# Output products of nine units from float32 with sums to three one-pass products of split halves, in a cross-attention kernel on one Trainium2 core

## The chip, the core and the metric

The kernel runs on one core of a Trainium2 chip (trn2). The metric is the device time in microseconds of one execution. Five engines work beside each other, each through its own queue in order: TensorE (PE, matrix products into the PSUM banks; weight loads are listed apart as PEld), VectorE (DVE), ScalarE (ACT), GpSimd (POOL) and SyncE (SP, which here only issues transfers).

## The reference

Inputs are `x` [2, 2048, 640], a context [2, 128, 384] and eight weights. The last 4 context rows are the adapter's tokens, the first 124 the text.

```python
query = hidden_states @ Wq
hs = _mha(query, enc @ Wk, enc @ Wv)              # 8 heads of 80, 124 text keys
ca_q1 = einsum('btc,th->bch', ca, Wq_ca)[:, indices, :]   # 384 channels spread to 2048
ca_hs1 = _mha(ca_q1, residual, residual)          # 2048 x 2048 scores, 384 distinct rows
ca_hs2 = _mha(ca_hs1 @ Wq, ca @ Wk_ca, ca @ Wv_ca)  # 4 keys
out = (hs + ca_hs2) @ Wout + b_out + residual
```

All of it is float32. The part that changes is the last line's product with `Wout`, [4096, 640] by [640, 640].

## The kernel before, in words

The 4096 tokens are cut into 8 blocks of 512 (for queries) and 16 units of 256 (for scores, probabilities and output); unit `m` is the second half or the first of block `m // 2`. The stages that matter here are these.

The adapter (`adapter`, `contract`, `second`) runs one chain per batch: scores `s` into a four-bank PSUM tile, a maximum on DVE (`mx`), scores again the other way round, an exponential on ACT (`ea`), and an accumulation `acc` on PE against `y_sb`. Only after the second batch's last `acc` are `y_sb` and the four-bank tile free; the latter becomes four more PSUM banks, eight in all.

For each unit, `text_scores` forms scores `sc` from the queries, `softmax` makes probabilities that go out to DRAM and come back turned (`kept`, then `pT`), `hidden` forms the hidden rows `ph` (three groups: chunks 0 and 1, chunks 2 and 3, chunk 4) from `pT` and the values, and `text_out_fast` multiplies them with `Wout` in steps `po`, each of which DVE adds to the residual rows (`x_more` or `last_rows`, which already hold `x` plus the bias). `stored` writes the rows out.

`text_out_fast` treats two token tiles by two pairs of 128-row chunks by two column halves of 320 as a 2x2 block product and forms it with seven products in place of eight, from sums of the hidden rows (`s1` to `s4`, on DVE or POOL) and of `Wout` (`wout_sums`, four tiles in the room of `Wq`, made once after the last query). The fifth chunk is multiplied plainly, four products. A product is two chunks wide for the seven, one for the fifth. Every product is float32. `Desk.matmul` issues a float32 product that fills the array as four strips of 32 columns, unless the instruction before filled the whole array; the printed records show each strip as two instructions. The last unit's last chain is split in two halves of 160 columns, each stored by itself.

Room limits: the hidden rows of a unit with their sums take one of three sets (`hs_sets`), and `pT` has two buffers, both made from tiles that earlier stages give up.

The order of all work is written out by hand of a planner: `ORDER` is a list of task numbers, one for each step, with a letter (`a`, `v`, `g`) where the engine is chosen there. `Desk.run` walks it and pins each instruction at its place in its engine's queue. Generators (`text`, `adapter` and so on) yield the steps; a `Room` is a count of free buffers, and a step that takes one from it can only stand in the order after the step that gives it. So `ORDER` sets the queues; waits between engines are semaphores made from the tiles that instructions read and write.

Of the kernel before, what the change touches and what calls it, by code (L numbers as in the profile page):

```python
# [45 lines left out]
class Do:  # L46
# [4 lines left out]
    def __init__(self, engine, fn, after=None, needs=(), frees=(), marks=()):  # L51
        self.engines = (engine,) if isinstance(engine, str) else engine
        self.fn, self.after, self.needs, self.frees, self.marks = fn, after, needs, frees, marks
        self.slots, self.value = [], None
# [12 lines left out]
class Desk:  # L67
# [3 lines left out]
    SIDES = {"a": "ACT", "v": "DVE", "g": "POOL"}  # L71
# [3 lines left out]
        2 2 2 2 2 2 36 0 0 0 4 4 0 0 0 0 0 0 0 0 4 0 0 111a 6 6 6 0 4 6 4 2 2 2 2 2 2 2 4 113a 107 108 109 110 4 6  # L75
        114a 115a 3 6 3a 3 116v 4 6 3a 3 3v 6 3 8 8 7 7 7 2 15 15 15 11 15 15 12 8 7 0 0 118a 8 5 15 15 15 15 10 7
        117a 15 7 8 7 7 7 120a 9 1 119v 8 6 121a 7 7 7 7 122a 7 7 124v 9 123v 125a 126a 8 8 127 8 9 8 36 5 128 8 8 8 5
        9 9 9 129 5 130 15 36 15 15 131 9 9 14 14 9 14 14 14 14 9 14 6 112 136a 133a 135v 134v 14g 137 36 112 11 112
        15 14 15 36 14 12 14g 36 138 138 138 36 138 138 12 12 12 36 144v 145v 12 36 36 11a 9 9 9 139 11 9 9 9 140 143a
        9 146a 12 13 101 17 106 140 140 140 140 141 18 6 140 140 140 140 142 106 132 132 16 17 147g 148g 132 101v 142  # L80
        132 101v 101g 101g 101g 39 152 152 152 152 152 152 151 17 17 36 36 156a 142 142 142 18 18 18 18 18 18 18 18
        132 142 16 151 152 36 36 142 16 16 157a 43 151 152g 149g 152 16 132 16 101v 101 18 16 16g 36 159 159 16 36 158
        36 101g 150g 101g 17 160a 159 159 16 151 161a 16g 155 18 18 18 152 162 36 153 36 18 158 158 18 158 155 17 155
        153 36 20 20 19 163 159 159 163 163 21 21 171 163 142 142 158 172 164 163 163 36 21 21 172 172 172 172 21 43
        154 36 154 175 175 165 159 36 175 175 175 175 19 19 19 159g 166g 167g 159 36 36 170 39 181a 36 170 21 21 21 21
        172 172 172 19 20 19 19 182 177 176 177 182 175 19g 19 177 177 159 173 36 20 183a 170 20 36 168g 182 182 182
        182 172 19 184a 20 178 170 178 182 169g 175g 17 21 21 21 21 21 21 22 19g 177 174 177 185 23 182g 36 36 185 185
        186a 185 185 175 24 24 24 24 24 175 24 174 174 24 24 188 24 174 187 185 36 22 47 22 22 22 192 22 180 194 179
        36 180 192 192 192 192 22 192 22g 182 190 174 182 36 179 180 36 195 192 196 36 47 174 174 174 158 20 23 202 23
        23 24 24 24 197 22 197 198g 192g 199v 36 192 36 24 201g 24 206a 197 197 197 22 200g 197 23 202 23 208 51 207a  # L90
        208 174 189 208 208 208 208 197 197g 22g 36 209 209 36 202 205 209 214a 209 192 132 197 189 158 189 189 189
        197 132 189 202 36 215a 209 205 189 209 36 216 55 36 203 205 209 217 217 24 209g 36 26 26 217 217 217 217 209
        217 27 27 27 27 27 158 209 210 27 212 27 204 36 204 203 218 51 36 36 225 224 219g 220g 222g 221g 217g 36 193
        226 226 223 228 230a 223 228 36 226 226 226 226 232a 229 193 217 132 158 217 158 189 23 189 191 191 191 191 27
        55 231v 36 36 233v 229 223 226 193 193 193 234 234 226g 36 226 235 234 234 234 234 25 26 229 234 36 236 36 36
        27 191 226 191 191 191 191 27 211 36 227 223 227 237 27 238 234g 234 25 59 239 239 25 25 27 27 27 27 239 239
        239 239 36 211 36 211 132 211 211 177 36 26 59 26 36g 241 241 211 211 211 211 213 29 29 241 241 241 247 239
        243v 240 251v 25 36 36 36 26 244g 247 36 252 252 254a 36 247 36 252 252 30 234 213 56 177 30 30 30 30 213 213
        213 25 239g 241 241 239 239 240 177 245g 241g 242 249 36 36 252 253 252 255a 253 247 249 253 253 36 253 36 25
        256v 253 36 63 252 193 252 252 40 213 28 252 36 44 30 30 30 30 193 262 262 257 246g 240 241 250 263 241 177 25  # L100
        240 213 262 262 262 262 36 67 36 36 252 213 240 30 30 30 264 30 264 30 250 252 250 36 30 262 265 262g 262 264
        264 213 36 252 252 31 252 29 31 36 252 264 264 31 36 67 36 31 193 193 258 260 193 262 259 259 10 259 36 60 26
        33 33 33 33 252 252 252 29 36 29 252 29 32 268 32 31 33 267 267 33 33 259 266 266 259 264 264g 269g 270g 264
        266 266 36 266 266 268 36 36 268 268 268 63 252 266 252 252 252 252 276 268 276 266v 267 31 33 264 267 274 273
        276 276 252 282a 36 36 36 252 273 36 283 283 284v 273 36 276 276 36 36 283 283 248 36 248 259 242 259 259 283
        283 271g 272v 276 31 242 285v 273 36 36 31 267 32 259 31 283 36 283 266 286 287v 33 31 283 28 36 31 28 28 36
        31v 252 28 283 281 71 36 283 276v 289 283 281 261 261 261 261 261 261 25 28 266 277 28 261 36 290 33 283 290
        288 33 36 281 283 290 290 36 290 290 33 291 33 276 33 33 32 36 75 28 25 276 25 36 261 283 28 35 35 68 283 283
        290 25v 292 292 290g 242 242 290 292 292 292 261 292 25 25 32 32 275 298 292 36 298 283 36 283 34 293v 294g
        25v 298 298 75 36 292g 298 298 301 295g 301 290 292 36 280 242 280 242 275 275 275 292 302 288 275 28 301 301  # L110
        301 301 28 28g 301 304 279 242 71 279 242 242 305 306 242 305 305 305 305 305 297 103 35 242 283 35 242 242
        283 283 307 288 242 102 275 68 296g 66 66 31 31 31g 36 36 275 275 275 299 68 68 28 11 310v 301v 307 35 242 64
        314 29 283 314 283 28 35 315 301 314 28g 316 283 48 283 283 309 317a 242 242 297 309 283 313 242 313 318a 313
        242 314 314 309 313 297 316 316 305 242 242 288 288 301 10 305g 32 316 278 278 278 316 313a 320a 308 297 308
        316 305 242 323 319 242 324 242 34 34 34 34 313 325 68 68 68 105 103 104 104 267 48 79 242 332 242 48 48 34 46
        46 278 34 321 34 278 305 332 311g 328g 330g 329g 68 68 335a 68 242 336a 331g 312g 339g 340g 333g 341g 338g 34
        102 105 40 38 38 34 48 48 40 48 278 68 288 337a 332 332 332 332 79 242 344 242 348 332 344 242 346 348 346 344
        344 242 242 345 344 242 344 344 348 278 348 34 348 278 278 348 52 332g 332 347 344 242 345 83 242 349 349 242
        349 349 349 349 345 345 349 347 48 242 352a 48 48 48 334g 359 34g 242 242 300 44 300 34 332 40 40 40 44 44 40
        300 44 44 44 351 288 300 300 349g 355g 349 349 288 42 240 240 42 34 354a 353a 356g 34g 357g 343g 358g 342g 242  # L120
        360 83 242 360 360 365 359 365 242 365 365 365 365 359 359 362 362 365 242 361 359 242 242 300 104 361 360 359
        242 40 359 40 44 242 359 365g 363g 40 367a 300 40 300 369a 368a 300 372g 365 373g 371a 87 348 242 380 380 44
        242 242 242 381a 44 384v 374v 380 382a 380 380 52 44 242 242 242 380 364g 385g 375g 376 376 378 377 387 378
        387 376 387 387 376 379 387 376 379 288 240 50 52 288 52 240 242 52 242 52 242 242v 242 366 240 365 52 50 377
        380 380g 348g 393g 392g 327 387 376 242 377 387 376 242 242 242 391 303 303 303 303 303 380 377 376 327 267
        387 327 327 380 267 391 52 52 242 391 391 242 52 52 327 391 60 327 396v 397v 403 303 303 386v 383v 403 399v
        400g 401v 242 398a 91 407 407 242 391 303 303 322 35 64 391 407 407 407 407 403 391 242 389 407 327 395 403
        403 403 242 242 242 391 322 327 267 322 267 322 322 327 402v 407g 407 407 391 403 404 242 389 403 242 91 64 60
        327 64 64 391 322 391 391 391 242 404 404 408 408 348 322 408 408 242 408 408 404 390 348 64 64 58 409 370 408
# [53 lines left out]
    def run(self):  # L183
        for entry in self.ORDER.split():
# [7 lines left out]
            for room, i in op.frees:  # L192
                room.give(i)
            for k in op.marks:
                self.event(k).known = True
# [44 lines left out]
def kernel(  # L240
# [1897 lines left out]
    for m in range(UNITS):  # L2138
        begin(text(m))
# [33 lines left out]
```

## Time and profile before

| | |
|---|---|
| median of 3 runs | 566.56 us (564.76 to 568.67) |
| span of the profiled execution, first to last instruction | 562.6 us |
| PE busy | 554.5 us, 99% |
| DVE, ACT, POOL busy | 386.4, 265.7, 198.4 us |
| granted TensorE clock | 1.000 |
| moved by transfers | 101.48 MB |

The profile is of one execution. Its own time is not listed beside its span; the median of the runs is 4.0 us above the span. A record of PE lasts from its start to a modelled end, and records overlap; so the distance from one start to the next tells what an instruction costs when PE is full. A row of a group gives line, engine, operation, `out<-in` with the shapes and a count, then the busy time, the mean duration of one in ns, and the idle time of the engine just before with what ended it. `128*32` is rows by columns of the array that an instruction uses. float32r operands are printed as f32 on PE and as fp32r where another engine writes them.

### The profile page before, as it was taken

The numbers are of one execution on the slowest core, as the hardware profiler recorded it, in microseconds if no ns is written. First come the engines' busy times: TensorE is split into PE (matmuls) and PEld (weight loads), VectorE is DVE, ScalarE is ACT, GpSimd is POOL, SyncE is SP. The second block draws the span as 40 slices with busy tenths as digits, with TensorE's granted clock in tenths as the row PEclk, the third lists the DMA queues.
The fourth block names the chain that finished last, engine by engine and source line by source line (L and its number), as shares of the span: only waits on it lengthen the run. The fifth ranks groups of instructions, "written<-read, shape, count | busy, mean of one in ns | idle before, by whom it ended". The sixth has DMA issues, their size and how long they took to land.

```text
span 562.6 us, 18845 instructions
## 1 busy us (share of the span) xinstructions
PE 554.5 (99%) x8088; PEld 314.4 (56%) x8088; DVE 386.4 (69%) x622; ACT 265.7 (47%) x733; POOL 198.4 (35%) x211
## 2 busy tenths in 40 slices
PE   9999999999999999999999999999999999999997
PEld 8563445456555555555465445455545666666664
DVE  1457999999996564579999998655635655555534
ACT  3122645445338898886525424579878230100100
POOL 7002534434524523013559364512330513321310
PEclk9999999999999999999999999999999999999999
DMA  8994769774877889455568895758853687688603
GB/s 264 240 172 127 154 119 161 165 169 141 162 198 163 179 249 172 140 170 172 170 138 248 217 236 133 241 163 255 252 165 108 181 186 192 150 262 229 203 28 142
DMA packets 151699, 101.48 MB, mean 180 GB/s; under 512 B 86492, under 2 KB 130156, under 8 KB 151616
## 3 DMA queue, kind: packets, MB, share of 16 engines
q1 hardware_dynamic: 150848, 99.88, 69.6%
q8 instruction: 64, 1.05, 0.8%
q0 software_dynamic: 768, 0.40, 0.4%
q14 instruction: 19, 0.16, 0.1%
HBM read 61.34 MB, written 38.90 MB: 178 GB/s over the span
## 4 chain that ended last, share of the span: by engine, by line
PE 91%; DVE 3%; DMA 3%; ACT 1%; SPq 1%; POOL 1%; issue 0%; ACTq 0%; DVEq 0%
PE po L211 26%; PE pq L211 25%; PE acc L211 8%; PE sc L211 7%; PE ph L211 7%; PE s L211 7%; PE pq_first L211 3%; PE pyz L211 3%; DVE mx L226 2%; PE pk L211 1%; PE unread L215 1%; DMA zb<-z 1%; DMA x_more<-in_x_dram 1%; DMA first_rests<-away 1%; SPq L236 1%; PE pt_wq L219 1%
## 5 line engine op out<-in xcount | busy, mean ns | idle before, releaser
L226 DVE TENSOR_REDUCE mx<-s 128x4 f32<-128x2048 f32 x48 | 109.2, 2275 | 2.5 <-PE s L211 2.4
L226 ACT ACTIVATE p<-sc,m 128x124 f32<-128x124 f32 x256 | 89.5, 374 | 32.2 <-DVE m L226 32.2
L226 ACT ACTIVATE ea<-s 128x2048 f32<-128x2048 f32 x48 | 90.4, 1884 | 26.5 <-PE s L211 26.2
L226 POOL TENSOR_TENSOR p<-p,r 128x992 f32<-128x992 f32 x28 | 51.9, 1857 | 132.9 <-DVE r L226 126.1
L211 PE MATMUL po<-wout_sums,hs 128*32 128x320 f32 (+1 forms) x1012 | 77.8, 433 | 0.5 <-DVE x_more L226 0.5
L211 PE MATMUL po<-wout_sb,hs 128*32 128x320 f32 (+2 forms) x972 | 77.1, 429 | 0.0
L226 DVE TENSOR_TENSOR x_more<-x_more,po 128x320 f32<-128x320 f32 x72 | 33.7, 480 | 42.6 <-PE po L211 42.6
L226 ACT ACTIVATION_READ_ACCUMULATOR p<-sc,m 128x1 f32 x256 | 55.4, 217 | 0.0
L211 PE MATMUL pq<-xt,wq_sb 128*32 128x256 f32 x896 | 54.3, 381 | 0.5 <-DVE q L226 0.5
L211 PEld LDWEIGHTS po<-wout_sums,hs 128*32 128x32 f32 (+1 forms) x1012 | 37.5, 110 | 29.7 <-issue 1.6
L211 PEld LDWEIGHTS po<-wout_sb,hs 128*32 128x32 f32 (+1 forms) x972 | 36.7, 111 | 27.4 <-issue 0.9
L211 PE MATMUL acc<-ea,y_sb 128*32 128x384 f32 (+2 forms) x768 | 50.4, 384 | 0.0
L226 DVE TENSOR_REDUCE m<-sc 128x4 f32<-128x496 f32 x64 | 40.8, 663 | 13.6 <-PE sc L211 13.4
L226 POOL TENSOR_TENSOR hs<-hs 128x256 f32<-128x256 f32 x35 | 27.5, 790 | 63.5 <-DVE hs L226 54.7
L211 PE MATMUL ph<-pT,vpad 128*32 128x256 f32 x768 | 46.7, 380 | 0.2 <-ACT p L226 0.2
L226 DVE TENSOR_TENSOR last_rows<-last_rows,po 128x320 f32<-128x320 f32 (+1 forms) x57 | 26.4, 473 | 24.8 <-PE po L211 24.7
L226 DVE STREAM_TRANSPOSE eb<-p 128x1024 f32<-128x1024 f32 x32 | 39.5, 1234 | 5.3 <-POOL p L226 3.3
L211 PEld LDWEIGHTS pq<-xt,wq_sb 128*32 128x32 f32 x896 | 27.5, 110 | 22.9 <-issue 5.5
L226 ACT COPY hs<-ph 128x512 f32<-128x512 f32 (+1 forms) x23 | 12.1, 541 | 58.9 <-PE ph L211 58.6
L211 PE MATMUL pq<-xt,wq 128*32 128x512 f32 x320 | 38.8, 595 | 0.0
L211 PEld LDWEIGHTS sc<-kmain,q 64*128 64x128 f32 x512 | 31.8, 187 | 11.9 <-issue 7.5
L211 PE MATMUL sc<-kmain,q 64*128 64x124 f32 x512 | 37.5, 283 | 0.2
(197 smaller groups left out, 792.3 us busy)
## 6 DMA issues: line engine op xcount, KB each, us to landing
kept<-eb SPq DMA_DIRECT2D x32, 512.0 KB
pT<-kept SPq DMA_DIRECT2D x48, 256.0 KB
landing<-away SPq DMA_DIRECT2D x60, 128.0 KB
xi<-in_x_dram SPq DMA_DIRECT2D x28, 256.0 KB
x_more<-in_x_dram SPq DMA_DIRECT2D x18, 320.0 KB
out_dram<-x_more SPq DMA_DIRECT2D x18, 320.0 KB
last_rows<-in_x_dram SPq DMA_DIRECT2D x14, 320.0 KB
y<-yt SPq DMA_DIRECT2D x16, 256.0 KB
```

Source lines behind the costliest of these rows:

```text
L211: self.pin(self.nc.tensor.matmul(out[strip], lhsT[:, strip], rhs, **kw))
L215: self.pin(self.nc.tensor.matmul(out, zeros, zeros, start=True, stop=True))
L219: self.pin(self.nc.tensor.transpose(out, in_, ident))
L226: return lambda *args, **kw: self.pin(getattr(engine, what)(*args, **kw))
L236: self.pin(self.nc.sync.dma_start(out, in_))
```

## The change

Units 0 to 4, 6 and 7 (`BY_SUMS`) keep `text_out_fast`, without the split at the end. Units 5 and 8 to 15 use the new `text_out`. Each float32 number is split in a top part of 12 bits and a remainder; both are float32r, which PE multiplies in one pass. With `top`, `low` (the remainder) and `mix` (their difference, scaled), three products give the full product: top by top, low by low, mix by mix, all accumulated in one bank and scaled once when DVE adds them to the residual. `Wout` is split by `wout_part` in five chunks of [128, 640], five steps each; the parts lie in rooms that the adapter's `zop`, `y_sb`, `yz`, the late tiles and `kmain` give up. The hidden rows are split in `hidden_parts` when they leave PSUM. An output of 128 tokens by 320 columns is one step of 15 matmuls, four such steps a unit, and no float32r matmul is cut into strips.

`hs_sets` goes from three sets to two; three sets of parts (`k_sets`) are added, one from two query slots, two more when the seven units by sums are done. `pT` gets two further buffers, from the tiles `ea0` and `ea1`, when the second batch's adapter rows are out. Bookkeeping (what marks a step done, when a room grows) is moved from side effects into steps of their own, which issue nothing. In `halves_away` both ACT copies now come ahead of both DVE subtractions. `ORDER` is new from end to end, 2366 entries for 2241; it was laid out by the planner with disturbed timings.

```diff
     def matmul(self, out, lhsT, rhs, **kw):
         rows, cols = lhsT.shape
-        wide = rows > 64 and cols > 64 and self.mode != (P, P)
+        wide = rows > 64 and cols > 64 and self.mode != (P, P) and lhsT.dtype == F32
...
+    BY_SUMS = (0, 1, 2, 3, 4, 6, 7)
+    UNDER, UP, DOWN = 1.0 - 2.0**-13, 2.0**12, 2.0**-12
+    ACROSS = -DOWN / (1.0 + DOWN)
...
-        yield from text_out_fast(m)
+        yield from (text_out_fast if m in BY_SUMS else text_out)(m)
...
     def take_pT():
...
+        yield Do("NONE", lambda *z: None, [("o2", B - 1)], needs=[(eas, 2)], grows=[(pTs, 2)])
...
+    def wout_parts():
...
+        yield Fork(one(Do("NONE", lower, [("acc done", B - 1, u) for u in range(2)], marks=["wout lows"])))
...
+        yield Fork(one(Do(
+            "NONE", mixed_in, ["wout lows"] + [("sc", m, k) for m in range(UNITS) for k in range(2)],
+            needs=[(yzs, 1)], marks=["wout mixes"],
+        )))
...
+    def wout_part(c):
+        top = w_parts["top"][c]
+        yield Do(ANY, lambda: top_of(top, wout_sb[:, c]), marks=[("wout top", c)])
+        op = yield Do(
+            ADDS, lambda: minus(w_parts["low"][c], wout_sb[:, c], top.bitcast(F32)), ["wout lows", ("wout top", c)],
+        )
+        low = w_parts["low"][c]
+        yield Do(ANY, lambda: times(low, UP), marks=[("wout up", c)])
+        yield Do(
+            ADDS, lambda: minus(w_parts["mix"][c], top.bitcast(F32), low.bitcast(F32)), ["wout mixes", ("wout up", c)],
+        )
+        yield Do(ANY, lambda: times(w_parts["mix"][c], ACROSS), marks=[("wout mix", c)])
...
+    def hidden_parts(m, c0, n, hs, ph, s, at):
...
+        yield Do(EITHER, lambda: top_of(cols("top"), src), [at], marks=[("hs top", m, c0)])
+        yield Do(
+            "DVE", lambda: minus(cols("low"), src, cols("top", True)), frees=[(banks, s)], marks=[("hs low", m, c0)],
+        )
...
+        op = yield Do(("DVE", "ACT"), scaled)
...
+    def out_part(m, i, u, hs):
+        def product(s, kinds=("top", "low", "mix")):
+            po = bank(s[0], f"po_{m}_{i}_{u}")
+            steps = [(k, c) for k in kinds for c in range(NCH)]
+            for n, (k, c) in enumerate(steps):
+                matmul(
+                    po[:, :HALF], hs[k][c - c % 2][:, c % 2, P * i : P * (i + 1)],
+                    w_parts[k][c][:, HALF * u : HALF * (u + 1)],
+                    start=(n == 0), stop=(n == len(steps) - 1),
                 )
...
+            desk.v_scalar_tensor_tensor(t, po[:, :HALF], 1.0 + DOWN, t, ALU.mult, ALU.add)
```

In `hidden_parts`, `scaled` writes `mix` in one DVE step (`low` times -4096 plus `top`), or `low` times 4096 on ACT with a subtraction on POOL or DVE behind it.

More of the change, by code (lines that the diff above doesn't have):

```diff
@@ L1170, in queries_fast @@
         )
[L1171 to L1184 removed]
+        yield Fork(read_all(n))
         def chain(n, c, steps):
@@ new lines, in times, with lower, mixed_in @@
+    def times(t, factor):
+        if desk.engine == "ACT":
+            desk.a_activation(t, t.bitcast(F32), AF.Identity, scale=factor)
+        else:
+            (desk.g_tensor_scalar if desk.engine == "POOL" else desk.v_tensor_scalar)(
+                t, t.bitcast(F32), factor, None, ALU.mult
+            )
+    ANY, ADDS = ("ACT", "DVE", "POOL"), ("POOL", "DVE")
+    def wout_parts():
+        yield Do("NONE", lambda: None, [("zop", B - 1, sb, 1) for sb in range(NSB)])
+        tops, lows, mixes = w_parts["top"], w_parts["low"], w_parts["mix"] = [], [], []
+        def lower():
+            t = const.tile([P, 6, H], F32R, tag="y_sb", name="wout_low")
+            lows.extend(chunks(t[:, :NCH]))
+            mixes.append(t[:, NCH])
+        yield Fork(one(Do("NONE", lower, [("acc done", B - 1, u) for u in range(2)], marks=["wout lows"])))
+        def mixed_in(y):
+            mixes.extend([
+                cap.tile([P, H], F32R, tag="yz", name="wout_mix_1"),
+                late["pool"].tile([P, H], F32R, tag="rests", name="wout_mix_2"),
+                late["pool"].tile([P, H], F32R, tag="landing", name="wout_mix_3"),
+                const.tile([P, H], F32R, tag="kmain", name="wout_mix_4"),
+            ])
+        yield Fork(one(Do(
+            "NONE", mixed_in, ["wout lows"] + [("sc", m, k) for m in range(UNITS) for k in range(2)],
+            needs=[(yzs, 1)], marks=["wout mixes"],
+        )))
+        for c in range(NCH - 1):
+            yield Do(
+                "NONE", lambda z, c=c: tops.append(cap.tile([P, H], F32R, tag=f"zop{z[0]}", name=f"wout_top_{c}")),
+                needs=[(zops, 1)],
+            )
+            yield Fork(wout_part(c))
+        yield Do(
+            "NONE", lambda: tops.append(const.tile([P, H], F32R, tag="wq4", name="wout_top_4")), ["last query"]
+        )
+        yield Fork(wout_part(NCH - 1))
@@ L2027, in text_out_fast @@
         one_h, both_h, end_h = of1, of2, [("hsT", m, 4)]
-        left = {"sums": 8, "products": 4}
         ready = [("xr", m, k) for k in range(2)]
@@ L2053, in product @@
                     return to
+                end = k == len(steps) - 1
                 op = yield Do(
-                    "PE", product, after + at + ready, needs=[(banks, 1)] if k == 0 else []
+                    "PE", product, after + at + ready, needs=[(banks, 1)] if k == 0 else [],
+                    marks=[("products", m, n)] if end else [],
                 )
@@ L2095, in stored @@
+    ends = {}
+    spans = (0, HALF), (HALF, H), (0, H)
     def stored(m, k, u, added):
```

443 lines of the change are left out of this document (260 added, 183 removed).

## The prediction

> **What bounds the kernel now.** I read the page first, for the engine that is never free.
>
> ```profile
> span 562.6 us, 18845 instructions
> PE 554.5 (99%) x8088; PEld 314.4 (56%) x8088; DVE 386.4 (69%) x622; ACT 265.7 (47%) x733; POOL 198.4 (35%) x211
> PE 91%; DVE 3%; DMA 3%; ACT 1%; SPq 1%; POOL 1%; issue 0%; ACTq 0%; DVEq 0%
> PE po L211 26%; PE pq L211 25%; PE acc L211 8%; PE sc L211 7%; PE ph L211 7%; PE s L211 7%; PE pq_first L211 3%; PE pyz L211 3%; DVE mx L226 2%; PE pk L211 1%; PE unread L215 1%; DMA zb<-z 1%; DMA x_more<-in_x_dram 1%; DMA first_rests<-away 1%; SPq L236 1%; PE pt_wq L219 1%
> ```
>
> TensorE (PE) is busy for 99% of the span and carries 91% of the chain of waits; the largest single item on that chain is `po`, the output products that the change rewrites. Busy is not the same as streaming, so the table by stage comes next. I cut it at 437 us, where the last adapter work ends and only scores of a late tile, hidden products (`ph`) and output products (`po`) are left.
>
> ```profile
> core 0: us, PE busy (x) PEld busy (x) DVE busy (x) ACT busy (x) POOL busy (x), PEclk, DMA share, GB/s
> 45.00:180.00 135.00, 133.65 (x1988) 70.92 (x1988) 123.55 (x157) 66.64 (x251) 54.75 (x43) 1.00 0.71 156
> 180.00:345.00 165.00, 163.00 (x2425) 86.96 (x2418) 129.69 (x167) 106.11 (x280) 71.27 (x63) 1.00 0.76 190
> 345.00:437.00 92.00, 92.00 (x1453) 50.02 (x1449) 49.51 (x87) 68.74 (x143) 26.38 (x20) 1.00 0.65 187
> 437.00:559.00 122.00, 121.98 (x1885) 76.37 (x1875) 64.95 (x136) 12.73 (x38) 33.25 (x35) 1.00 0.64 178
> ```
>
> From 437 to 559 us PE has no idle time at all, VectorE (DVE) is busy 65 of 122 us, and the transfers use 0.64 of their engines. In that stage the time is PE time and nothing else. Earlier PE is as full, but DVE is at 123.55 of 135 us in the stage from 45 to 180, so that there two engines are close to their limit. How much of the output work lies in the late stage:
>
> ```profile
> 437.00:562.60 125.60, 99.81 (x1434) 58.32 (x1434) 36.49 (x81) 1.00 0.62 175
> ```
>
> This is the row of `po` alone: 1434 matmul records. One output product of 128x128 by 320 columns is issued as eight (four column strips of 32, two instructions each), so these are 179 products, ten units of 18 less one. Ten of the sixteen units do their output products after 437 us; the nine that are changed (5 and 8 to 15) are among them, and unit 4 is the tenth.
>
> **The change part by part: the products.** Price of one old product, from a stretch of the timeline with nothing in between:
>
> ```profile
> 449.75 6.13 PE L211 MATMUL po<-wout_sums,hs 128*32 128x320 f32 x88
> 455.67 1.29 PE L211 MATMUL po<-wout_sb,wout_sums 128*32 128x320 f32 x16
> 456.75 1.51 PE L211 MATMUL ph<-pT,vpad 128*32 128x256 f32 x24
> ```
>
> From 449.75 to the start of `ph` at 456.75 are 7.00 us for 104 instructions, 13 products: 0.538 us each. The strip form hides its weight loads completely. A unit had 7 sum-products of two chunks and 4 fifth chunks, 18 products: 9.69 us; nine units 87.2 us.
>
> A new unit has 4 outputs x 3 kinds x 5 chunks = 60 matmuls of full 128x128 weights by 320 columns in `float32r`. The trace has no full-array matmul of that type, so its price is put together from three sets of rows. First the streaming rate:
>
> ```profile
> L211 PE MATMUL pq<-xt,wq_sb 128*32 128x256 f32 x896 | 54.3, 381 | 0.5 <-DVE q L226 0.5
> L211 PE MATMUL pq<-xt,wq 128*32 128x512 f32 x320 | 38.8, 595 | 0.0
> L211 PE MATMUL s<-zop,cop x192: 462/497/504, 45.3 to 343.4; 32*128 32x512 f32 x192
> L211 PE MATMUL s<-cop,zop x384: 213/352/442, 177.4 to 434.4; 32*128 32x384 f32 x64, 32*128 32x128 f32 x64, 32*128 32x256 f32 x64
> ```
>
> An `f32` instruction takes 214 ns more for 256 more columns, 0.84 ns a column. The one-pass kind (`zop` and `cop` are `float32r`, which the trace prints as f32) takes at most 442 ns at 384 columns and 497 in the median at 512: 55 ns for 128, 0.43 a column, half, and an `f32` product needs two such instructions. So 320 columns stream in 133 to 138 ns. Second, whether the weight load hides under it:
>
> ```profile
> 59.81 0.66 PE L211 MATMUL sc<-krest,rests 64*128 64x124 f32 x8 [0.40 <-ACT rests L226]
> 177.43 0.51 PE L211 MATMUL s<-cop,zop 32*128 32x384 f32 x8
> L211 PE MATMUL sc<-krest,rests x256: 268/272/323, 59.8 to 443.8; 64*128 64x124 f32 x128
> ```
>
> Eight one-pass matmuls of `sc` run as four pairs, each pair with new 128-column weights: the last ends 0.66 us after the first began and itself takes 0.272, so it begins after 0.39 us. Take off the 0.05 by which the first waits longer (0.323 less 0.272), and three steps fill 0.34 us, 0.11 a step, where 124 columns stream in 0.053. The step is the load. In the second row the two rounds of `s` (384, then 128 columns) take 0.51 us: a load of 0.11, streams of 0.16 and 0.05 and the 0.16 by which a record outlasts its stream (0.213, the shortest, less the 0.053 of 128 columns) make 0.48; a second load in the open would make it 0.59. So a one-pass load costs about 0.11 us and goes on while the matmul before it streams. Third, for full-array weights:
>
> ```profile
> 34.09 3.93 PE L211 MATMUL pk<-ctxT,w_k 128*128 128x248 f32 x18
> L211 PE MATMUL pk<-ctxT,w_k 128*128 128x248 f32 x18 | 3.9, 373 | 0.0
> ```
>
> Eighteen of these, each with its own load, advance by (3.93 - 0.37)/17 = 0.209 us, and 248 columns stream in 0.208: the loads are hidden there too. With a load of 0.11 under a stream of 0.133 I take 0.136 us for a new matmul (0.133 to 0.140): 8.16 us a unit, 73.4 for nine. The products give back 87.2 - 73.4 = **13.8 us**, all of it in the stage where PE is the bound.
>
> [...]
>
> **Mode changes.** `ph` stays in 128x32 strips, so PE now goes from strips to full array and back.
>
> ```profile
> 438.17 1.26 PE L211 MATMUL po<-wout_sb,hs 128*32 128x320 f32 x16
> 439.37 0.55 PE L219 MATMUL pt_acc<-ident,accs 128*128 128x128 f32 x3
> ```
>
> Two products stream in 1.08 us from 438.17, to 439.25; the full-array transposes begin at 439.37: 0.12 lost, and the first load on top, at most 0.11. The way back costs the same drain and a load of a quarter of the columns, 0.03: up to 0.38 us a pair. In the new order the hidden products of two units mostly stand together, so there are five or six pairs; each `ph` group alone would make 27. I take **2 us**, ends 1.6 and 10.
>
> **Work on the other engines.** Of each changed unit go four sums, one copy each for three groups of `ph`, and four of eight additions; in come three `top`, three `low`, three `mix` and four additions.
>
> ```profile
> L226 DVE TENSOR_TENSOR q<-q,pq 128x512 f32<-128x512 f32 x28 | 18.6, 671 | 4.7 <-PE pq L211 4.6
> L226 DVE TENSOR_TENSOR x_sums<-xt,x_sums 128x512 f32<-128x512 f32 x2 | 1.4, 685 | 0.0
> L226 DVE TENSOR_TENSOR x_more<-x_more,po 128x320 f32<-128x320 f32 x72 | 33.7, 480 | 42.6 <-PE po L211 42.6
> L226 ACT ACTIVATE zop<-zb,low_z 128x512 fp32r<-128x512 f32 x8 | 5.9, 738 | 11.3 <-DMA zb<-z 11.3
> ```
>
> DVE: `low` 2.5 times 0.671, `mix` 2.5 times 0.685, four additions of 0.48: 5.3 us, in a unit that takes PE 8.2 and some 2.7 of `ph` (half of its records are the 1.51 us above, less the 0.16 of drain). DVE is half used, and `top` (0.74 on ACT) is off it mostly. A chain `ph`, `top`, `low`, `mix` is about 2.1 us long and the order runs another unit's products over it, so I cost it at nothing; without that cover it is 2.1 us, nine times. A `ph` bank is held by `top` and `low`, 1.4 us instead of one copy, with eight banks at hand. The four `pT` buffers move transfers earlier and add none: 0.64 of the transfer engines becomes about 0.71 in a stage ten per cent shorter, still no bound.
>
> **The halves of Wout.** Twenty-five steps of 128x640, five for each chunk, are new. `low` needs the room of `y_sb`, free only when the last accumulation is read at about 439 us, and no new unit can start its products before all five chunks have gone through subtract, scale, subtract, scale.
>
> ```profile
> L226 DVE TENSOR_TENSOR last_rows<-last_rows,bias 128x640 f32<-128x640 f32 x6 | 6.2, 1040 | 1.7 <-DMA last_rows<-in_x_dram 1.7
> L226 POOL TENSOR_TENSOR x_more<-x_more,bias 128x640 f32<-128x640 f32 x12 | 18.7, 1559 | 26.3 <-DMA x_more<-in_x_dram 26.2
> ```
>
> Ten subtracts at 1.04 (DVE) to 1.56 us (POOL) and ten scalings of about 0.9 on ACT (0.738 for 512 columns) make some 10 to 12 us with three engines. What PE has meanwhile: unit 4's products, 9.7 us, a late tile of scores, and `ph` of the first units, three sets of 2.7 us. That is more than 17 us, so little shows. I take **1 us**; with unit 4 used up too early it is up to 5. What is queued behind these steps is, on DVE, the last softmax and unit 4's additions, and on POOL bias additions that the late units need; PE waits for both only through those units. In the query stage, `halves_away` now makes both copies before both subtractions; its bank is held until the last subtraction as before, and I cost it at nothing.
>
> **Front and end.** The order is new everywhere. Until 437 us the same products run, so I take **0**. A gain by less idle time is bounded by the idle time that is there: 3.4 us of PE from 45 to 437 (135 - 133.65 and 165 - 163 in the rows above), and a few mode changes. A loss is not bounded so tightly, since DVE at 92% in the stage from 45 to 180 can make PE wait if work is laid badly; I allow 6. At the end a last addition of 160 columns becomes one of 320.
>
> ```profile
> 559.03 0.32 DVE L226 TENSOR_TENSOR last_rows<-last_rows,po 128x160 f32<-128x160 f32 x1 [0.49 <-PE po L211]
> ```
>
> From its start at 559.03 to the end are 3.6 us of addition and store; 0.48 instead of 0.32 adds **0.2 us**.
>
> Sum: 562.6 - 13.8 + 2 + 1 + 0 + 0.2 = 552.0 us of span. The median before, 566.56, is 4.0 above the span of the profiled execution, so the time is **556 us**.
>
> **The rivals.** (1) The gain is given back on the way: several `ph` groups change the mode singly (up to 7 us more), the halves of Wout leave PE idle at 440 us (up to 4 more), and the new front loses some. For it: PE had no slack to lose, and the chain of four new steps replaces one copy. Against it: DVE is only half used late. Half to all of these costs gives 561 to 569 us.
>
> (2) Slower: the full-array one-pass load is not hidden. For it: the only one-pass rows are of 32 or 64 rows, and there the loads of 128 columns are as long as 0.11 us, near the 0.133 of the stream. Price 540 x 0.11 = 59 us, to about 615. It decides early: from 20 ns of exposed load a matmul the forecast's gain is gone (10.6 us over 540), and from 30 ns the kernel is over 1% slower. Against it: the `s` and `pk` rows.
>
> (3) Better than forecast: the new front also removes its idle time and mode changes; 4 to 5 us more, 547 to 551.
>
> **How the numbers follow.** One per cent, 5.7 us, is about what can be told from no change. Forecast (551 to 561) 0.56; given back (561 to 569) 0.24; load exposed, or an order so bad that it costs over 16 us, 0.11; better 0.09. Faster by over 1% (below 560.9): 0.56 + 0.09 and 0.02 from the lower edge of the second, 0.67. Within 1%: 0.22. Slower: 0.11. The range is 548 to 568: it leaves out the slow rival (0.11) and the outer edges of the better and the given-back case (0.03 each). It takes in 10 us of mode changes, or 5 of stall with the front's 6, but not all at once.
>
> **What would show it.** `po` of the late units as full-array rows of about 300 ns each, advancing by 0.136 us; 540 of them with 73 to 76 us busy. If they advance by 0.19 or 0.24, the load was exposed and the forecast falls. The last `pt_acc` near 437 to 440 us shows the front right; much later, or with PE idle before it, shows the order to blame. Idle PE before the first full-array `po`, released by `wout_mix`, would be the junction. PE busy near 540 us with idle under 10 would confirm the sum.

## The result and the profile after

The changed kernel takes 580.25 us in the median, the kernel before 566.60 beside it on the same chip: 1.025 times as long, interval 1.0205 to 1.0296. Forecast were 556 us and a gain. The change is slower by 2.5 per cent, and 580 lies above the range of 548 to 568. The profile of the changed kernel is of the fastest of its four executions, 577.39 us; the others took 579.55 to 583.24.

The head of the page of the changed kernel: span, busy time and its share for each engine, and the chain of waits by engine.

```profile
span 575.7 us, 17256 instructions
PE 553.1 (96%) x7290; PEld 339.0 (59%) x7290; DVE 404.0 (70%) x624; ACT 274.1 (48%) x746; POOL 206.7 (36%) x206
PE 59%; DMA 13%; DVE 12%; SPq 8%; ACT 3%; issue 3%; POOL 1%; DVEq 0%; ACTq 0%; POOLq 0%
```

PE was busy for 99% of the span and is for 96%; on the chain of waits it fell from 91% to 59%, and transfers, DVE and SP's queue took its place. The sum of busy time is nearly that of before (553.1 for 554.5), with 798 matmul records fewer. So the matmuls did go, and the time came back, partly as idle time. The table by stage shows where. The stages are cut at the last turn of the accumulations (`pt_acc`), where the work of the adapter ends:

```profile
45.00:180.00 135.00, 131.43 (x1926) 69.11 (x1920) 122.99 (x153) 65.54 (x242) 56.92 (x52) 1.00 0.80 176
180.00:352.00 172.00, 167.53 (x2484) 89.09 (x2482) 130.01 (x167) 108.34 (x292) 73.93 (x60) 1.00 0.68 175
352.00:448.80 96.80, 94.60 (x1472) 51.66 (x1469) 55.19 (x99) 70.51 (x148) 29.60 (x21) 1.00 0.70 187
448.80:571.00 122.20, 115.81 (x1087) 98.78 (x1085) 75.56 (x130) 20.10 (x48) 35.85 (x24) 0.99 0.61 160
```

Idle time of PE up to the turn: 3.6, 4.5 and 2.2 us, 10.3 in all. In the kernel before it was 1.4, 2.0 and 0 in the rows that the prediction shows. Behind the turn PE idles for 6.4 us, where it idled for nothing. The last turn itself, in the rows of the matmuls that write `pt_acc` (first and last start), of the kernel before:

```profile
L219 PE MATMUL pt_acc<-ident,accs x12: 272/273/329, 221.4 to 439.6; 128*128 128x128 f32 x12
```

and of the changed kernel:

```profile
L229 PE MATMUL pt_acc<-ident,accs x12: 272/273/329, 228.5 to 448.8; 128*128 128x128 f32 x12
```

About the same work of PE runs ahead of it (24 more instructions of `sc` and 16 more of `po`, 48 fewer of `ph`), and it comes 9.2 us later: 9.2 us of the loss lie ahead of the stage that the change was meant for. What PE waited for in the changed kernel (total, times, longest):

```profile
PE s L221 <- DVE mx L236: 3.1, 5, 1.2
PE po L221 <- DVE x_more L236: 2.5, 2, 1.4
PE ph L221 <- DVE ks L236: 2.2, 1, 2.2
PE ph L221 <- DMA pT<-p: 1.4, 2, 1.1
PE po L221 <- DVE ks_mix L236: 1.2, 1, 1.2
```

No wait is above 2.2 us. They are spread over the scores of the adapter (`s`, five times, twice in the kernel before), the halves (`ks`), additions (`x_more`) and the transfer of the second rows of the probabilities.

Behind the turn, the new products. One output of a unit is fifteen matmuls; the timeline shows the first of each, and between the two rows lie six outputs, 90 matmuls, with nothing else on PE:

```profile
498.63 0.89 PE L221 MATMUL po<-wout_top,ks 128*128 128x320 f32 x5
...
511.83 0.89 PE L221 MATMUL po<-wout_top,ks 128*128 128x320 f32 x5
```

13.20 us for 90 matmuls are **0.1467 us each**, where the prediction had 0.136. The longest stall, in the timeline of PE, and the granted clock around it (the column behind the five engines, in the windows of the second fence):

```profile
486.90 1.07 PE L221 MATMUL ph<-pT,vpad 128*32 128x256 f32 x16
490.17 4.27 PE L221 MATMUL ph<-pT,vpad 128*32 128x256 f32 x44 [2.20 <-DVE ks L236]
```

```profile
487.90:490.20 2.30, 0.10 (x8) 0.06 (x5) 1.39 (x2) 0.60 (x1) 0.00 (x0) 1.00 0.52 161
490.20:493.60 3.40, 3.40 (x40) 2.24 (x44) 1.38 (x2) 0.93 (x2) 0.00 (x0) 0.60 0.51 143
493.60:496.30 2.70, 2.70 (x44) 1.61 (x36) 2.30 (x4) 0.65 (x2) 0.00 (x0) 0.87 0.57 167
```

PE idles 2.2 us while one group of `ph` goes through `top`, `low` and `mix` with no product over it, and behind that runs at a clock of 0.60 for 3.4 us and 0.87 for 2.7: 1.4 and 0.3 us more, 3.9 in all for one uncovered chain. The last addition, in the timeline of DVE, leaves 4.5 us to the end of the span:

```profile
571.18 0.49 DVE L236 SCALAR_TENSOR_TENSOR last_rows<-po,last_rows 128x320 f32<-128x320 f32 x1 [1.29 <-PE po L221]
```

### The profile page after: what moved, and what is told of

It reads as the page before. It is cut to its first block, busy times and chain, and to the rows that moved or that the text cites. A ratio compares the mean times of both kernels' runs of the same rounds, so it can differ in the third digit from the quotient of the medians.

```text
span 575.7 us, 17256 instructions
## 1 busy us (share of the span) xinstructions
PE 553.1 (96%) x7290; PEld 339.0 (59%) x7290; DVE 404.0 (70%) x624; ACT 274.1 (48%) x746; POOL 206.7 (36%) x206
## 4 chain that ended last, share of the span: by engine, by line
PE 59%; DMA 13%; DVE 12%; SPq 8%; ACT 3%; issue 3%; POOL 1%; DVEq 0%; ACTq 0%; POOLq 0%
PE po L221 20%; PE pq L221 12%; SPq L246 8%; PE acc L221 6%; PE sc L221 5%; PE s L221 4%; PE ph L221 4%; DVE mx L236 3%; PE pq_first L221 3%; DMA landing<-away 3%; DMA last_rows<-in_x_dram 2%; DMA zb<-z 1%; PE pyz L221 1%; DMA pT<-kept 1%; ACT ea L236 1%
## 5 line engine op out<-in xcount | busy, mean ns | idle before, releaser
L221 PE MATMUL pq<-xt,wq_sb 128*32 128x256 f32 (+1 forms) x884 | 54.7, 381 | 0.1
L221 PEld LDWEIGHTS pq<-xt,wq_sb 128*32 128x32 f32 (+1 forms) x884 | 27.6, 110 | 21.9 <-issue 3.9
L221 PEld LDWEIGHTS ph<-pT,vpad 128*32 128x32 f32 x768 | 26.0, 112 | 23.3 <-issue 6.1
L221 PE MATMUL po<-wout_sums,hs 128*32 128x320 f32 x436 | 34.8, 435 | 2.5 <-DVE x_more L236 2.5
L221 PE MATMUL po<-wout_sb,hs 128*32 128x320 f32 (+1 forms) x446 | 36.6, 435 | 0.5 <-ACT hs L236 0.5
L221 PE MATMUL po<-wout_low,ks 128*128 128x320 f32 x204 | 35.7, 309 | 0.0
L236 ACT ACTIVATE ks<-ph 128x512 fp32r<-128x512 f32 (+1 forms) x17 | 9.0, 542 | 52.4 <-PE ph L221 52.2
L236 POOL TENSOR_TENSOR x_more<-x_more,bias 128x640 f32<-128x640 f32 x12 | 19.2, 1605 | 40.2 <-DMA x_more<-in_x_dram 40.2
L221 PE MATMUL po<-wout_top,ks 128*128 128x320 f32 x180 | 32.6, 311 | 0.2 <-DVE ks L236 0.2
L221 PEld LDWEIGHTS acc<-ea,y_sb 128*32 128x32 f32 x768 | 21.1, 109 | 17.4 <-issue 8.4
```

Of the source, the lines that this page charges most:

```text
L221: self.pin(self.nc.tensor.matmul(out[strip], lhsT[:, strip], rhs, **kw))
L236: return lambda *args, **kw: self.pin(getattr(engine, what)(*args, **kw))
```

## The experiments

**The price of the new matmul by itself.** A kernel with no other work issues series of one-pass matmuls with full 128x128 weights, each with its own load: 60 each of 320, 512, 256 and 128 columns, then `f32` products, then 60 of 320 columns that load the same weights again. The attention is left out of it.

```diff
+    loop("full_320", 1, rr, wr, 320, False, 60)
+    loop("full_512", 2, rr, wr, 512, False, 60)
+    loop("full_256", 3, rr, wr, 256, False, 60)
+    loop("full_128", 4, rr, wr, 128, False, 60)
+    loop("full_f32", 5, rows, w, 320, False, 32)
+    loop("same_320", 6, rr, wr, 320, False, 60, same=True)
```

> This kernel leaves the whole attention out: it copies 512 rows of x to all rows of the output and, beside that, runs loops of 60 matmuls with new weights each, to price the one-pass product by itself. The changed kernel advances by 0.146 us per full-array one-pass matmul of 320 columns where the prediction took 0.136. Theory A, a fixed cost of 13 ns on each matmul beside the stream: 512 columns advance by 0.226, 256 by 0.120, 128 by 0.11 (the load). Theory B, the load sets the pace at 0.146: 256 and 128 columns also take 0.146, 512 take 0.216. Theory C, the one-pass stream is slower per column (0.456 ns): 512 take 0.234, 256 take 0.117. If the 13 ns come from loading new weights, the loop that loads the same weights each time takes as long (each load is still issued); if they come from traffic of the other engines in the changed kernel, 320 columns take 0.136 here. The float32 full-array loop should take 0.269 per instruction, as in the strips.

Groups by shape (busy time, mean duration of one in ns):

```profile
L56 PE MATMUL b<-wr,rr 128*128 128x320 f32 x120 | 18.3, 312 | 0.0
L56 PE MATMUL b<-w,rows 128*128 128x320 f32 x64 | 17.4, 433 | 0.0
L56 PE MATMUL b<-wr,rr 128*128 128x512 f32 x60 | 13.8, 389 | 0.0
L56 PE MATMUL b<-wr,rr 128*128 128x256 f32 x60 | 7.4, 283 | 0.0
L56 PE MATMUL b<-wr,rr 128*128 128x128 f32 x60 | 6.8, 274 | 0.0
```

Busy time less the duration of the last, by the count less one, is the step: (13.8 - 0.389)/59 = 0.227 us at 512 columns, 0.121 at 256, 0.111 at 128. For 320 it is (18.3 - 0.624)/118 = 0.150 over both series, and (6.47 - 0.31)/42 = 0.147 in a stretch of 43 in the middle of one. From 256 to 512 columns the step grows by 0.107 us, 0.417 ns a column, which is also half of the prediction's 0.84 for `f32`. By it 512 columns stream in 0.213, 320 in 0.133, 256 in 0.107 and 128 in 0.053.

So a one-pass matmul with a full-array load takes about 14 ns beside its stream at 256, 320 and 512 columns, and only at 128 columns is the step more than twice the stream; there the load, 0.11 us, is taken to be the bound. An `f32` instruction of the same shape takes (17.4 - 0.433)/63 = 0.269, its stream of 0.267 and 2 ns. The first theory of the expectation holds: the 13 ns belong to the form, neither to the weights being new (the series that loads the same weights again advances by 0.151) nor to the other engines, and the load is hidden. In column strips of 32 the loads of the old products hid at no such cost (0.538 us a product for two streams of 0.267); column strips of 32 or 64 were not tried with this type.

**The order alone.** The arithmetic of the kernel before, in the order of the changed kernel up to the last step of the adapter, behind it in the order of before. Only `ORDER` differs from the kernel before.

```diff
     ORDER = """
-        ...
+        ...
     """
```

> The kernel before with its own products for all sixteen units, but with the work up to the last adapter step laid out in the changed kernel's order (the tail in the order of before). Theory 1, the order itself costs the 9.2 us by which the last adapter transposes came later: they come at about 449 us here too, and the time is about 576 us, 1.6% over before. Rival, the front was slowed by what the change adds there (the top halves of Wout on POOL, copies ahead of subtractions, two sets of hidden rows in place of three): the transposes come at 440 and the time is 566 to 568 us.

579.91 us, 1.0247 times before (1.0182 to 1.0313). The turn of the accumulations and the waits of PE:

```profile
L217 PE MATMUL pt_acc<-ident,accs x12: 272/273/328, 229.6 to 457.3; 128*128 128x128 f32 x12
```

```profile
PE s L209 <- DVE mx L224: 4.5, 6, 2.0
PE ph L209 <- DMA pT<-p: 3.6, 1, 3.6
PE s L209 <- ACT ea L224: 1.7, 3, 1.4
```

With not one product changed the order makes the kernel as slow as the change. The turn comes 17.7 us late, and the same waits show (scores for `mx`). So the order alone is enough to delay the front, and the new work is not needed for it. Behind the turn this kernel takes 123.0 us, as the kernel before does: its whole loss lies ahead of the turn. Of the 17.7 us, 13 are more idle time of PE and 1.7 a low clock behind the stall of 3.6 us. They are not to be held against the 9.2 us of the changed kernel: this profile is of an execution of 581.97 us, and in the medians the two kernels lose about as much (13.5 and 13.7 us).

**The old front, the new tail merged in.** The new products in the kernel before, with everything up to the adapter's last step in the order of before and the rest taken greedily in the order of the changed kernel. The bookkeeping steps and the regrouped copies of `halves_away` stay out, as in the five planned kernels below.

```diff
+    BY_SUMS = (0, 1, 2, 3, 4, 6, 7)
...
-        yield from text_out_fast(m)
+        yield from (text_out_fast if m in BY_SUMS else text_out)(m)
```

> The changed output products for units 5 and 8 to 15, with everything up to the last adapter step in the order (and with the bookkeeping and copies) of the kernel before; behind it the changed kernel's order of the tail. Theory 1: the last adapter transposes come back to about 440 us, and the time is 571 us (580.25 less 9.2), still slower than before by some 0.8%, because the tail keeps its stalls and its 0.146 us a product. Rival, a front that is as fast only hands its waits on to the tail: 576 to 580 us. If the tail's stalls came from the new front's state (which buffers were free), it would fall to 560 to 566 us.

592.84 us, 1.0495 (1.0434 to 1.0556): slower still.

```profile
PE pt_acc L222 <- DVE ks L229: 6.8, 1, 6.8
PE po L214 <- DVE last_rows L229: 5.6, 1, 5.6
PE ph L214 <- DMA pT<-p: 5.5, 3, 2.0
PE po L214 <- DVE ks L229: 3.9, 2, 3.3
```

The last scores were back at 433.9 us (434.4 before), so the front was mended; but the last turn waited 6.8 us for DVE, which by the profile had steps on `ks` ahead of what the turn needs. PE stood still at the junction for 5.6 and 6.8 us, and four more times for 1.6 to 3.3 us by 534 us. The time is above all three outcomes expected. This neither confirms nor refutes that a good order exists. It shows that this merge of two orders makes no good junction.

**A third of the new products left out.** The changed kernel without the products of `top` with `mix`; all the splits stay. This tells whether PE is the bound behind the junction.

```diff
-        def product(s, kinds=("top", "low", "mix")):
+        def product(s, kinds=("top", "low")):
```

> The changed kernel without the third kind of product (top times mix, five of the fifteen matmuls of each out product, 180 in all): the output lacks the cross terms. All the splits, scalings and mixes on ACT, DVE and POOL stay. Theory 1 (after its junction the end of the changed kernel is bound by TensorE, at 0.147 us per one-pass matmul): 180 x 0.147 = 26.5 us less, span about 550 instead of 576. Rival (the halves and additions on DVE and ACT set the pace of the last 110 us, and TensorE only fills in): less than half of that goes, span above 562, and the waits of TensorE for DVE tiles grow by what is not gained.

560.07 us in one execution, span 558.4, so 17.3 us less, where PE alone would have given 180 x 0.147 = 26.5. Its largest wait:

```profile
PE ph L221 <- DMA pT<-p: 12.2, 4, 5.2
PE s L221 <- DVE mx L236: 3.3, 6, 1.0
```

Of the 17.3 us, 1.4 lie ahead of the turn, which came at 447.4 us instead of 448.8; so 15.9 of the 26.5 us taken from PE come off the stage behind it. In exchange 12.2 us of waiting for probability rows appear (1.4 in the changed kernel). PE is the first bound of that stage. The next, some 16 us behind it, are the transfers of probability rows, and not the halves on DVE. In the three waits for them behind the turn the transfer engines were at 0.97, 0.82 and 0.35, so that in the last at least it is when they were issued, not what the engines can move. That is neither of the two outcomes expected.

**Planned orders.** The front of before is kept to 432 us. Behind it each step gets a place by a plan with the durations measured in both traces. The first plan, once with nine one-pass units and once with eight (unit 5 by sums, which gives PE some 10 us more of its own work at the junction):

```diff
-    BY_SUMS = (0, 1, 2, 3, 4, 6, 7)
+    BY_SUMS = (0, 1, 2, 3, 4, 5, 6, 7)
```

> The same arithmetic as the changed kernel (nine units by one-pass products), the instructions up to 432 us in the order of the kernel before, and the rest ordered by a plan made with the measured durations of both traces. Theory 1 (the order of the first 440 us costs 9 us, the tail's stalls the rest, the fixed 13 ns per matmul stays): last adapter scores at 434 and last turn of the accumulations at about 440 us as before, one stall of 4 to 5 us where units of the second half wait for the second rows, last addition at 560 to 562, span 564 to 567, time 566 to 571: some 2 per cent below the changed kernel and level with the kernel before. Rival (the change's own work on DVE, ACT and POOL is what delays the front and the junction, whatever the order): the last turn again past 447 us, stalls of 10 us and more, time 575 or above.

> As the one before, but unit 5 keeps the products by sums (eight units by one-pass products), so that TensorE has about 10 us more work of its own while the second rows and the halves of Wout are made. Theory 1: no stall over 1 us at the junction, last addition at 557 to 559, span 561 to 563, time 562 to 567, level with the kernel before or up to 1 per cent below it. Rival (each one-pass unit gains nothing once its 60 matmuls, two mode changes and halves are paid): slower than the run with nine units by the 1 us that unit 5 costs more, or no better.

593.49 us (1.0504, 1.0476 to 1.0533) and 591.18 (1.0455, 1.0405 to 1.0504): both far off. The turn was in place with both (442.0 and 440.8 us). Of the one with nine, the window behind the junction and SP's queue around it (start, length, transfers issued):

```profile
460.00:480.00 20.00, 0.63 (x12) 0.15 (x4) 7.14 (x10) 2.58 (x5) 5.97 (x5) 0.57 0.97 199
```

```profile
439.00 0.52 SPq L239 DMA_DIRECT2D kept<-eb  x1
456.11 0.35 SPq L239 DMA_DIRECT2D out_dram<-x_more  x1
...
459.86 0.38 SPq L239 DMA_DIRECT2D p<-rows  x1
460.67 2.26 SPq L239 DMA_DIRECT2D pT<-kept  x4
462.98 0.84 SPq L239 DMA_DIRECT2D x_more<-in_x_dram  x2
463.92 8.56 SPq L239 DMA_DIRECT2D pT<-kept  x8
473.08 3.87 SPq L239 DMA_DIRECT2D pT<-p  x4
```

From 439.5 to 456 us SP issues nothing, since its queue stands at a store that waits for additions. The loads of twelve quarter megabytes for three units then go out at once, and the last rows (`pT<-p`), which all of them need, stand behind. PE is busy 0.63 of 20 us, with the transfer engines at 0.97. With eight units the same wait was 11.1 us. The plan had neither SP's queue in its order nor the transfers as a resource, and here they set the time. The 12.2 us of the run before are waits for the same rows; whether the queue made them too was not tried.

The second plan counts both, with the transfers at 225 GB/s (from 460 to 480 us the last two runs moved 199 and 230):

> Nine units by one-pass products, front in the order of the kernel before, and a new plan for the rest that also counts SP's queue in its order and the transfers of the probability rows at the 225 GB/s that the last two runs showed. Theory 1 (order of the front 9 us, tail stalls 8 us, fixed 13 ns per matmul; the transfers on SP's queue were what the last two plans had wrong): last turn of the accumulations at 440 to 441 us, waits for probability rows under 3 us in all, one stall of about 3 us before the first unit of the second half, last addition at 560 to 563, span 564 to 567, time 566 to 571, level with the kernel before. Rival (with nine units the junction cannot be filled in any order, since the halves of Wout, the second rows and their transfers need 15 us after the last accumulation): stalls of 8 us or more between 440 and 470, time 575 or above.

> The same plan with unit 5 by sums (eight units by one-pass products): TensorE has some 10 us more work of its own at the junction. Theory 1: no stall over 1 us after 440, last addition at 556 to 558, span 560 to 562, time 562 to 565, level with the kernel before or up to 0.8 per cent below it, and some 15 us below the changed kernel. Rival (a one-pass unit gains nothing over a unit by sums once everything is paid): no better than the kernel before, 567 or above, with no single stall to blame.

With nine units 567.55 us, 1.004 times before (1.0021 to 1.0058); with eight 564.44, 0.9986 (0.997 to 1.0003). Both times are within the forecasts of theory 1; the one large wait of each was longer than forecast (4.4 us for about 3, and 3.0 for under 1). The turn, and around the one large wait the timeline, of the plan with nine:

```profile
L222 PE MATMUL pt_acc<-ident,accs x12: 272/273/330, 220.3 to 441.3; 128*128 128x128 f32 x12
```

```profile
452.06 1.91 PE L214 MATMUL ph<-pT,vpad 128*32 128x256 f32 x32
458.35 4.48 PE L214 MATMUL ph<-pT,vpad 128*32 128x256 f32 x48 [4.38 <-ACT ks L229]
```

This is the arithmetic of the change, nine units of one-pass products, and it is 12.7 us faster than in the order of the change (1.004 times before for 1.025). One stall of 4.38 us remains, where the rows of the second batch, the halves of Wout and the first `ks` all fall due together; the 48 records behind it take 4.48 us, where 48 of the same take 2.80 in the last run below: 1.7 us of low clock. With eight units that stall was gone, and a wait of 3.0 us for the second rows of unit 11 was left. The last run lays the plan with eight units once more, with 2.6 us instead of 0.9 from the end of a transfer to its reader; both are figures of the plan, and no row here shows them:

> The plan with eight one-pass units laid once more, with 2.6 us instead of 0.9 from the end of a transfer to its first reader, since the one wait left in the last plan (3.0 us for the second rows of unit 11) came from there. Theory 1: that wait goes, last addition at 554 to 557, span 558 to 561, time 561 to 564, 0.3 to 0.9 per cent below the kernel before. Rival (the junction costs the same wherever the rows come, because the halves of Wout and the second rows bind there): another wait of 3 us or more between 440 and 475, time 564 to 567, no better than the last plan.

561.31 us, 0.9909 times before (0.9882 to 0.9935). The windows from the junction to the last product:

```profile
440.00:470.00 30.00, 29.90 (x455) 17.67 (x444) 25.97 (x43) 9.63 (x29) 26.73 (x20) 1.00 0.84 224
470.00:500.00 30.00, 29.59 (x276) 26.50 (x280) 16.86 (x29) 3.34 (x7) 9.73 (x7) 1.00 1.02 210
500.00:530.00 30.00, 30.00 (x314) 25.61 (x307) 21.36 (x38) 6.52 (x14) 6.76 (x5) 1.00 0.70 199
530.00:556.00 26.00, 26.00 (x179) 25.84 (x177) 11.12 (x20) 1.06 (x3) 5.38 (x4) 1.00 0.16 61
```

```profile
475.82 2.80 PE L214 MATMUL ph<-pT,vpad 128*32 128x256 f32 x48
```

PE idles 0.5 us in 116, at full clock. The junction is nearly full on the other engines too: DVE at 26 of 30 us, POOL at 26.7, transfers at 0.84 and then at 1.02. This version is 0.9 per cent faster than the kernel before and some 3 per cent faster than the change as it stands; it beats both.

## Why the prediction was wrong

The sum gave a span of 552.0 us; it was 575.7, 23.7 more. By the prediction's own steps:

| step | forecast | measured | difference |
| --- | --- | --- | --- |
| front, to the last turn | 0 | 448.8 for 439.6 | +9.2 |
| 540 new matmuls | 0.136 us each | 0.1467 | +5.8 |
| mode changes | 2 | 2.3 | +0.3 |
| junction and chains behind the turn | 1 | 6.4 idle, 1.7 of low clock | +7.1 |
| end, from the last addition | 3.8 | 575.7 - 571.2 = 4.5 | +0.7 |

They make 23.1 of the 23.7.

**"Front and end: until 437 us the same products run, so I take 0"** is the step that failed most. It named the danger (DVE at 92% from 45 to 180 us) and allowed 6 us in the range, but gave the order a price of nothing because the products stay. The order alone, with no product changed, cost 17.7 us to the turn in its profile and 13.5 us of the median time; the new products behind the old front had the turn back at 441 us. Of the 9.2 us the stages show 6.9 as more idle time of PE ahead of the turn. The rest is not idle time: PE is busy for 437.2 us up to the turn, where it was for 435.1, and why is open. Which steps of the order are to blame was not tried one by one. The regrouped copies of `halves_away` are not needed for it, since the kernel with the order alone has the old ones.

**"I take 0.136 us for a new matmul"** was mis-sized by 0.0107. The form was put together from a stream of one-pass rows in strips and from `pk`, a full-array row of `f32`. But the excess over the stream is 2 ns in an `f32` instruction and 14 in a one-pass one, so that the `f32` row could not show it, and the one-pass rows in strips were used for their rate alone. The products gave back 87.2 - 79.2 = 8.0 us instead of 13.8, 0.89 a unit.

The `pk` row was right that a full-array load hides, and with it the second rival's mechanism was wrong although its sign came true. Full-array loads of 0.11 us are hidden under streams of 0.107 us and more: at 256 columns the step is 0.121 us, where load and stream one after the other would take 0.218. What hides them, and where the 14 ns come from, no run here shows.

**"I take 1 us" for the halves of Wout and "I cost it at nothing" for the chain of halves.** The chain had its price (2.1 us without cover) and the order left it without cover at 487.9 us: 2.2 us idle. What the prediction did not have is what can follow an idle PE, here 1.7 us of low clock. At the junction itself, from the turn to the first new product at 462.9 us, PE idles 2.0 of 14.1 us, with DVE busy for 13.9 and POOL for 13.8. The prediction's count of cover there, "more than 17 us", was too high. Only one of the three sets of `ph`, that of unit 5, ran ahead of the first new product; the sets of the second batch wait for the second rows, which are made in the same 15 us and reach their place through SP's queue. The nine-unit plan kept 4.4 us of stall in the best order found, the eight-unit plan, with unit 5's products as cover, none. "Up to 5" as the upper end was right.

**"Still no bound" for the transfers** held for the change as it stands (1.4 us of waits, at 0.61 to 0.70 of the engines), but only by some 16 us, as the run with a third of the products left out shows; in the two first plans they and SP's queue were the bound.

**Mode changes** (2 against 2.3) were right: there are ten of them behind the turn, and the starts in the timeline of PE, less the streams, leave 0.3 to 0.5 us for a way into the full array (at 462.93 us 0.27 ahead of the first one-pass matmul and 0.10 over the first five) and about 0.1 for a way back. The first rival, given back on the way, was right in two of its three causes. It named the front and the halves, which cost, and single mode changes, which did not come; it stopped at 569 because it took half to all of each cost as forecast. The signs that the prediction named were the right ones: a `pt_acc` much later than 440 us with idle PE ahead of it was to blame the order, and did.

By the table the change would be worth, in an order without stalls, 8.0 us of products less 2.3 of mode changes, 5.7 us or 1 per cent. No run reached that with nine units (567.55 us is the best); the version with eight has 0.9 per cent.

## What to carry to other kernels

Where one engine is busy for 99% of the span, a new order of instructions is a term of the sum, and not of zero: price it by the last event of the stage that keeps its work, and keep the old order for that stage when only the end is changed. Price a matmul from rows of its own form and type; a stream rate from one form and a load from another leave out what the form adds (here 14 ns). When work is taken off the bound engine, list the next bound with its distance in us (here the queue that issues transfers, and the transfers), since a plan that knows only the compute engines runs into it.

## What the runs showed of the hardware

A one-pass `float32r` matmul with a full-array load costs 13 to 14 ns beside its stream from 256 to 512 columns, an `f32` instruction of the same shape 2 ns. In the changed kernel an idle time of PE of 2.2 us was followed by 3.4 us at a granted clock of 0.60 and 2.7 us at 0.87, in the second plan with nine units one of 4.4 us by a clock of 0.62 over the next 4.5 us; each cost 1.7 us beyond itself. But in these runs the length of a stall of 2 to 3 us does not tell whether that follows. The same 80 instructions of `ph`, in the second plan with eight units (first row) and in the merged orders of "The old front":

```profile
468.58 4.52 PE L214 MATMUL ph<-pT,vpad 128*32 128x256 f32 x80 [3.03 <-DMA pT<-p]
```

```profile
498.66 4.52 PE L214 MATMUL ph<-pT,vpad 128*32 128x256 f32 x80 [1.95 <-DMA pT<-p]
523.89 6.21 PE L214 MATMUL ph<-pT,vpad 128*32 128x256 f32 x80 [2.00 <-DMA pT<-p]
```

At the full clock they take 4.52 us, after 3.03 and 1.95 us of idle time, and 6.21 after 2.00, as after the 2.20 us in the changed kernel. Nor did a low clock follow the 3.3 us in the merged orders: from 520 to 560 us the granted clock was 0.96 there, which is 1.6 us, and the row of 6.21 us accounts for that. Three longer idle times were followed by one: 3.6 us in the order alone (a clock of 0.99 over the 172 us from 180 to 352, 1.7 us), 6.78 us in the merged orders (three `pt_acc` instructions in 0.90 us, where three take 0.55 in the changed kernel), and 11.08 us in the first plan with eight units (144 instructions of `ph` in 10.47 us; 96 take 5.39 in the changed kernel). So 2.00 and 2.20 us were enough, and 1.95, 3.03 and 3.3 were not.

In the last three planned kernels the transfers filled their engines from 470 to 500 us (1.02 to 1.04, 210 to 259 GB/s), and PE was busy beside them for 29.6 to 30.0 of the 30 us at a granted clock of 1.00.
